# A graph layer with segment maxima: x theta^T of the last 5120 nodes is made in the middle of the kernel and kept in HBM

## The chip, the cores and the metric

One core of one Trainium2 chip runs the whole layer. Its engines are TensorE (PE: matmuls and transposes into PSUM; PEld are its weight loads), VectorE (DVE), ScalarE (ACT), GpSimd (POOL, which also issues the gathers, indirect DMAs), and SyncE (SP, which only issues DMAs here). Each engine works through its own queue in order. The metric is the time of one execution on the device in microseconds (us). A profiled execution gives the trace from which all durations below come.

## The reference

```python
# x (6250, 256), src and dst (100000,), dst ascending; theta_w, phi_w (256, 256)
x_src, x_dst = x[src], x[dst]
e   = relu((x_dst - x_src) @ theta_w.T + theta_b + x_src @ phi_w.T + phi_b)
out = segment_max(e, dst, num_segments=6250)
out = where(isfinite(out), out, 0.0)
x   = layernorm(x + out)           # over the last axis, eps 1e-5
```

All edges of one destination share `x_dst @ theta_w.T` and the biases. With a = x theta^T + both biases (one row per destination) and b = x (phi - theta)^T (one row per source), the result before the layer norm is x + relu(a + max of b over the sources). So no matmul is needed per edge: the work is two products of 6250 x 256 by 256 x 256, and a maximum over 100000 rows of b.

## The kernel before

Nodes are split. Part 1 is the first 1130 nodes (nine tiles of at most 128), part 2 the last 5120 (40 tiles of 128). The edges of part 1 are taken by gathers; those of part 2 partly by matmuls with 0/1 matrices, the rest by gathers again. The stages, with the times they take in the profile:

- **Prep (40 to 148 us).** `x_transposed` (lines 742 to 750) transposes two tiles of x on TensorE and copies them from PSUM with ScalarE into a tile `x_t`; `b_of` (752 to 762) makes b from it, and b goes to HBM (`b_rows`). Meanwhile GpSimd gathers rows of x for the first groups of part 1's edges. `run` (683 to 696) takes running maxima over a group of eight steps on VectorE (line 688) and writes them to HBM (`maxima`, line 696) from SP.
- **Choice (148 to 262 us).** Sources are cut into 17 slots of 383 rows. `choice` (VectorE) picks for each node of part 2 at most one source per slot, `wanted` (1024 to 1031) transposes the picks and writes them to HBM (`chosen_rows`). The loop over `s0`, two slots a turn, also calls `next_group_1(1)`: the gathers of one group of part 1 (`b_rows`, without pauses here, `paced[0] = 0`), one `node_place`, and one fetch part.
- **Fetch parts (85 of them, 165 to 653 us).** `slot_part(s, c)` loads the picks of 1024 nodes (`want`, line 1061), makes 0/1 matrices `hot` from them on ScalarE (lines 1067 and 1068, two instructions a block; from `dve_hots[0] = DVE_HOTS` on, one of three blocks on VectorE, line 1065), and multiplies them with the slot's rows of b on TensorE (line 1075, 24 matmuls of 128 x 512). The results are copied (slot 0, line 1084, ScalarE) or maximised (later slots, line 1086, VectorE) into the accumulator `acc`, 128 x 2 x 5120: column n holds node n's maxima, transposed.
- **List (263 to 646 us).** What the choice left over is gathered from `b_rows`, eight steps a group, a pause (an `iota` of 160 columns, line 488) behind each gather (`paced[0] = 1`); `run` writes its maxima to `maxima_2`. Parts and groups are woven together in a fixed order.
- **End (654 to 744 us).** `rows_of` (1274 to 1319) takes shares of eight tiles, the last two of four: it loads x (`x_f`, ring of `X_RING`), gathers each node's maxima from HBM (line 512), and per piece of two tiles transposes x again (1292), copies it (`x_t`, 1294), makes a with theta and the bias (1299, 1302), for part 2 transposes `acc` back (1309) and takes the maximum with the gathered rows (1310), adds a (1311), and adds relu of it to x with a sum per row (1314). `normalise` (1321 to 1344) is the layer norm: squares on ScalarE (1328), root on both engines (418 to 424), x_f on ScalarE (1338), write of out from SP (1344). A class `Shares` weaves the norm of one share between the pieces of the next. One share of part 1, `LAST`, is done near the end of the fetch already.

Which instruction stands where in an engine's queue is decided by the scheduler of the framework at build time, from the order of the program and the buffers: a tile's ring (`bufs`) sets how many are in flight, and an instruction whose buffer is not free waits at the head of its queue.

Of the kernel before, what the change touches and what calls it, by code (L numbers as in the profile page):

```python
# [40 lines left out]
FP = mybir.dt.float32  # L41
# [6 lines left out]
ALU = mybir.AluOpType  # L48
# [4 lines left out]
P = 128  # L53
BIG2 = 3.0e38
EPS = 1e-5
STEPS = 8
# [17 lines left out]
SLOT_BITS = 9  # L74
P_BITS = 7
EARLY_STEPS = 6
X_RING = 5
STEPS_BITS = 3
OWN_LIST = 288
LIST_CHUNK = 232  # L80
# [2 lines left out]
PAD_WORD = 63 << 14  # L83
CARRY_GROUPS = 5
CARRY_AT = 9
FAR = 1000000.0
GENERAL_STEPS = 17
LOWEST = -1.0e30
# [10 lines left out]
def flat(t, offset, ap):  # L99

    return bass.AP(tensor=t.tensor, offset=t.offset + offset, ap=ap)
# [326 lines left out]
def gnn_kernel(ctx: ExitStack, tc: tile.TileContext, x, src, dst, theta_w, theta_b, phi_w, phi_b, out):  # L428
# [31 lines left out]
    maxima_2 = dram.tile([P * LIST + 1, D], FP, name="maxima_2")  # L460
    src_list = dram.tile([EDGES], I32, name="src_list")
    dst_list = dram.tile([EDGES], I32, name="dst_list")
    list_words = dram.tile([(P + 4) * OWN_LIST], I32, name="list_words")
    chosen_rows = dram.tile([NS, OWN], HF, name="chosen_rows")
    maxima_1t = maxima_1[: P * T1, :].rearrange("(p t) d -> p t d", t=T1)
# [106 lines left out]
    def misc():  # L572
        return ps_misc.tile([P, 2 * D], FP, name="ps")
# [136 lines left out]
    with (  # L710
# [28 lines left out]
                    nc.tensor.transpose(ps[:, 0, k, :], w_in[:, i, c, k * P : (k + 1) * P], ident)  # L739
                nc.vector.tensor_copy(weights[:, :, i, c * P : (c + 1) * P], ps[:, 0])  # L740

        def x_transposed(rows):
            w = rows.shape[1]
            ps = ps_t.tile([P, 2, KC, P], FP, name="ps_xt")
            for h in range(w):
                for k in range(KC):
                    nc.tensor.transpose(ps[:, h, k, :], rows[:, h, k * P : (k + 1) * P], ident)
            x_t = prep.tile([P, 2, KC, P], FP, name="x_t", bufs=3)
            nc.scalar.copy(x_t[:, :w], ps[:, :w])  # L749
            return x_t  # L750

        def b_of(to, rows):

            n = rows.shape[1]
            x_t = x_transposed(rows)
# [14 lines left out]
        for k, share in enumerate(shares(4)):  # L770
            n = share[2]
            x_q = x_in.tile([P, 4, D], FP, name="x_q")
            if share == LAST:
                nc.vector.memset(x_q[:, 0, :], 0.0)
            nc.sync.dma_start(present(x_q, *share), node_rows(x, *share))
            b_sb = b_out.tile([P, 4, D], FP, name="b_sb")
            for i in range(0, n, 2):
                w = min(2, n - i)
                b_of(b_sb[:, i : i + w, :], x_q[:, i : i + w, :])
            nc.scalar.dma_start(node_rows(b_rows, *share), present(b_sb, *share))  # L780
            if k == X_AFTER:
                x_group(of_x[0])
# [32 lines left out]
    place_2 = const.tile([P, TILES], I32, name="place_2")  # L815
    head_i = const.tile([P, 1], I32, name="head_i")
    carry_caps = const.tile([P, 2, P], FP, name="carry_caps")

    def node_place(j):
        cols = columns[:, j // Q1, :]  # L820
# [452 lines left out]
    def rows_of(part, j0, n, ps_tile):  # L1273


        share = part, j0, n
        x_f = x_ring.tile([P, STEPS, D], FP, name="x_f")
        if share == LAST:
            nc.vector.memset(x_f[:, 0, :], 0.0)
        nc.sync.dma_start(present(x_f, *share), node_rows(x, *share))  # L1280
# [2 lines left out]
        for k in range(n):  # L1283
            gather(m[:, k, :], maxima, places[:, j0 + k : j0 + k + 1])
        totals = work.tile([P, STEPS], FP, name="totals", bufs=3)

        def piece(k):
            w = min(2, n - k)
# [12 lines left out]
                    )  # L1301
                nc.tensor.matmul(a[:, i, :], pick, bias_terms, start=False, stop=True)
            some = m[:, k : k + w, :]
            if part == 2:
                ps = ps_tile().rearrange("p (i d) -> p i d", i=2)
                for i in range(w):
                    at = (j0 + k + i) * P
                    for c in range(KC):
                        nc.tensor.transpose(ps[:, i, c * P : (c + 1) * P], acc[:, c, at : at + P], ident)
                nc.vector.tensor_tensor(some, some, ps[:, :w, :], op=ALU.max)  # L1310
            nc.vector.tensor_tensor(some, some, a[:, :w, :], op=ALU.add)
            for i in range(k, k + w):
                y = x_f[:, i, :]
# [2 lines left out]
                )  # L1316
            yield

        return [piece(k) for k in range(0, n, 2)], normalise(part, j0, n, x_f, totals)

    def normalise(part, j0, n, x_f, totals):

# [58 lines left out]
    def fetch_parts(n):  # L1381
        for _ in range(min(n, len(parts))):
            slot_part(*parts.pop(0))

    def next_group_1(n):
        if groups_1:
            i = groups_1.pop(0)
            gathers = gather_group(i, b_rows)
            if i > X_GROUPS:
                run_1(i - 1, gathers)  # L1390
        if todo:
            node_place(todo.pop(0))
        fetch_parts(n)

    fill_table()
    paced[0] = 0
    for s0 in range(0, NS, BATCH_S):
        choice(s0)
        wanted(s0)
        next_group_1(1)  # L1400
    chunk_heads()
    dve_hots[0] = DVE_HOTS
    for i, _ in enumerate(list_pieces()):
# [83 lines left out]
```

## Time and profile before

| what | value |
|---|---|
| time, median of 3 runs (lowest to highest) | 749.13 us (747.54 to 750.01) |
| the profiled execution: time, span | 746.02 us, 744.2 us |
| TensorE busy | 650.4 us, 87% |
| VectorE busy | 641.4 us, 86% |
| GpSimd busy | 604.9 us, 81% |
| ScalarE busy | 492.7 us, 66% |
| moved by DMA | 164.84 MB, mean 221 GB/s |

The span is from the first to the last instruction in the trace; the time around it is 1.8 us. In the rows shown below, a page line by slice has 40 digits, each the busy share of 18.6 us in tenths (PEclk: the granted clock of TensorE in tenths of full speed). A row by window reads: from and to, length, then busy us (and instructions) of PE, PEld, DVE, ACT and POOL, then the granted clock, the busy share of the DMA engines, and GB/s. A row of a group reads: line, engine, operation, output <- input, shape, count | busy us, mean ns of one | idle time in front of them and what ended it. A row in order of time reads: start, duration, engine, line, operation, and in brackets the idle time before it with what ended it ("issue": nothing that the trace shows).

### The profile page before, as it was taken

The page shows a single profiled execution, that of the slowest core. Times are in us where ns is not written, and L with a number is a line of the kernel's source. Part 1 is how long each engine was busy: PE and PEld are TensorE (multiplying, and loading weights), DVE is VectorE, ACT ScalarE, POOL GpSimd, SP SyncE. Part 2 cuts the span into 40 slices and gives each one's busy share as a digit, 9 for nine tenths or more (in the row PEclk, how much of TensorE's full clock was granted, in tenths as well). Part 3 has the DMA queues.
Part 4 walks back from the last instruction along what each step waited for, and adds up shares of the span by engine and source line. Part 5 has one row for each costly group of instructions (what it writes and reads, how often), then busy time and mean ns, then how long its engine had stood idle before and what let it go on. Part 6 is the DMA issues. An engine that isn't in the chain of part 4 may idle for free.

```text
span 744.2 us, 10255 instructions
## 1 busy us (share of the span) xinstructions
PE 650.4 (87%) x3018; PEld 537.3 (72%) x3018; DVE 641.4 (86%) x1197; ACT 492.7 (66%) x700; POOL 604.9 (81%) x843
## 2 busy tenths in 40 slices
PE   1299999939777999999999999999999999589970
PEld 0288888726556788688888888888888888479970
DVE  6699999999997989598889989889799899768871
ACT  0144444459997777688777877877787775037885
POOL 7788987788887778888888888888888888648840
PEclk9599999959999999999999999999999999999995
DMA  6577745584677787968777777768768777625542
GB/s 207 144 244 244 248 159 193 176 286 151 209 239 256 239 254 231 356 211 267 230 235 223 261 243 251 228 223 251 262 205 261 229 222 250 224 101 180 180 173 116
DMA packets 55895, 164.84 MB, mean 221 GB/s; under 512 B 11835, under 2 KB 19796, under 8 KB 48500
## 3 DMA queue, kind: packets, MB, share of 16 engines
q1 hardware_dynamic: 32344, 98.76, 38.1%
q0 software_dynamic: 20944, 57.62, 27.5%
q10 hardware_dynamic: 2540, 7.69, 2.9%
q8 instruction: 27, 0.44, 0.3%
q14 instruction: 40, 0.33, 0.1%
HBM read 101.08 MB, written 63.74 MB: 221 GB/s over the span
## 4 chain that ended last, share of the span: by engine, by line
PE 52%; ACT 11%; DVE 5%; DMA 5%; POOL 3%; issue 2%; DVEq 0%; ACTq 0%; POOLq 0%; SPq 0%
PE ps_f L1075 49%; DMA want<-chosen_rows 4%; POOL g L512 3%; ACT x_f L1338 3%; ACT squares L1328 3%; ACT hot L1067 2%; ACT hot L1068 2%; DVE acc L1086 2%; PE ps_e L1299 1%; ACT acc L1084 1%; DMA g<-b_rows,src 1%; ACT x_t L1294 1%; DVE g L688 1%; DVE x_f L1314 1%; DVE g L1310 0%
## 5 line engine op out<-in xcount | busy, mean ns | idle before, releaser
L1075 PE MATMUL ps_f<-hot,terms 128*128 128x512 f32 x1960 | 458.0, 395 | 29.0 <-ACT hot L1068 15.6
L1075 PEld LDWEIGHTS ps_f<-hot,terms 128*128 128x128 f32 x1960 | 370.2, 190 | 113.1 <-ACT hot L1068 19.8
L512 POOL DMA_INDIRECT g<-b_rows,list_src x232 | 235.4, 1015 | 39.4 <-issue 35.6
L1067 ACT ACTIVATE hot<-want,minus_row 128x1024 fp32r<-128x1024 f16 x169 | 186.2, 1147 | 92.7 <-PE ps_f L1075 80.2
L1086 DVE TENSOR_TENSOR acc<-acc,ps_f 128x1024 f32<-128x1024 f32 x160 | 193.5, 1215 | 31.9 <-PE ps_f L1075 31.0
L688 DVE SCALAR_TENSOR_TENSOR g<-g,caps 128x256 f32<-128x256 f32 x376 | 180.0, 479 | 8.4 <-DMA g<-b_rows,src 5.2
L1068 ACT ACTIVATE hot<-hot 128x1024 fp32r<-128x1024 f32 x169 | 169.1, 1046 | 0.0
L512 POOL DMA_INDIRECT g<-b_rows,src x98 | 128.0, 1306 | 30.5 <-issue 25.3
L488 POOL IOTA pause<- 128x160 f32 x384 | 120.4, 314 | 5.5
L759 PE MATMUL ps_b<-weights,x_t 128*128 128x256 f32 x388 | 90.5, 388 | 1.3 <-ACT x_t L749 0.5
L759 PEld LDWEIGHTS ps_b<-weights,x_t 128*128 128x128 f32 x388 | 72.9, 192 | 14.4 <-ACT x_t L749 5.0
L512 POOL DMA_INDIRECT g<-in_x_dram,src x48 | 60.3, 1256 | 11.3 <-issue 7.1
L512 POOL DMA_INDIRECT g<-maxima,place x49 | 47.6, 972 | 24.6 <-issue 22.5
L1065 DVE TENSOR_SCALAR hot<-want,row_id 128x1024 fp32r<-128x1024 f16 x76 | 59.8, 788 | 6.4 <-DMA want<-chosen_rows 6.3
L1299 PE MATMUL ps_e<-weights,x_t 128*128 128x256 f32 x192 | 48.5, 380 | 0.3 <-ACT x_t L1294 0.2
L1299 PEld LDWEIGHTS ps_e<-weights,x_t 128*128 128x128 f32 x192 | 32.8, 190 | 3.9 <-ACT x_t L1294 0.8
L1294 ACT COPY x_t<-ps_e 128x512 f32<-128x512 f32 x24 | 13.7, 574 | 32.4 <-PE ps_e L1292 32.4
L762 ACT COPY b_sb<-ps_b 128x512 f32<-128x512 f32 (+1 forms) x25 | 14.4, 578 | 29.8 <-PE ps_b L759 28.0
L762 ACT COPY g<-ps_b 128x512 f32<-128x512 f32 x24 | 14.1, 586 | 29.8 <-PE ps_b L759 27.5
L1338 ACT ACTIVATE x_f<-x_f,r 128x256 f32<-128x256 f32 x49 | 25.3, 590 | 10.8 <-DVE r L1335 10.7
L749 ACT COPY x_t<-ps_xt 128x512 f32<-128x512 f32 (+1 forms) x49 | 26.1, 593 | 0.0
L1328 ACT ACTIVATE squares<-x_f,r 128x256 bf16<-128x256 f32 x49 | 24.2, 499 | 1.6 <-DMA g<-b_rows,list_src 1.0
(266 smaller groups left out, 502.2 us busy)
## 6 DMA issues: line engine op xcount, KB each, us to landing
maxima<-g SPq DMA_DIRECT2D x47, 1024.0 KB
want<-chosen_rows SPq DMA_DIRECT2D x85, 256.0 KB
x_q<-in_x_dram SPq DMA_DIRECT2D x12, 512.0 KB
b_rows<-b_sb ACTq DMA_DIRECT2D x12, 512.0 KB
x_f<-in_x_dram SPq DMA_DIRECT2D x5, 1024.0 KB
out_dram<-x_f SPq DMA_DIRECT2D x5, 1024.0 KB
raw<-b_rows SPq DMA_DIRECT2D x16, 256.0 KB
g<-b_rows,list_src POOLq DMA_INDIRECT x232, 4.3
```

The source lines that it names most:

```text
L488: return nc.gpsimd.iota(t, pattern=[[step, t.shape[1]]], base=base, channel_multiplier=per_partition, allow_small_or_imprecise_dtypes=True,)
L512: in_turn(nc.gpsimd.indirect_dma_start(out=out, out_offset=out_offset, in_=in_, in_offset=in_offset))
L688: one = nc.vector.scalar_tensor_tensor(g[:, k, :], last[part], caps[:, t : t + 1], g[:, k, :], op0=ALU.min, op1=ALU.max)
L759: nc.tensor.matmul(ps[:, h, :], x_t[:, h, k, :], weights[:, k, 0, :], start=(k == 0), stop=(k == KC - 1))
L1065: nc.vector.tensor_scalar(hot[:, b, :], want, row_id[:, b : b + 1], None, op0=ALU.is_equal)
L1067: nc.scalar.activation(hot[:, b, :], want, AF.Abs, bias=minus_row[:, b : b + 1], scale=1.0)
L1068: nc.scalar.activation(hot[:, b, :], hot[:, b, :].bitcast(FP), AF.Relu, bias=1.0, scale=-1.0)
L1075: nc.tensor.matmul(ps[:, w : w + 512], terms[:, part, b, h * P : (h + 1) * P], hot[:, b, w : w + 512], start=(i == 0), stop=(i == n - 1),)
L1086: latest_part[0] = nc.vector.tensor_tensor(to, to, ps, op=ALU.max).ins.name
L1299: nc.tensor.matmul(a[:, i, :], x_t[:, 2 * i + c, :], weights[:, c, 1, :], start=(c == 0), stop=False)
L1328: nc.scalar.activation(squares, x_f[:, k, :], AF.Square, bias=mean[:, k : k + 1], scale=1.0, accum_out=var[:, k : k + 1])
L1338: nc.scalar.activation(x_f[:, k, :], x_f[:, k, :], AF.Identity, bias=mean[:, k : k + 1], scale=inv[:, k : k + 1])
```

## The change

The transposed x of part 2's columns is no longer thrown away after b is made. `x_transposed` copies it into the accumulator, whose columns are free until slot 0 writes them. A new function `a_piece` makes a = x theta^T + biases of two tiles from there, copies it with ScalarE to SBUF, and writes it to HBM (`a_rows`) from SP. The loop of the choice calls seven pieces in each of its first turns (7, 7 and 6), behind `wanted` and ahead of `next_group_1`; its first turn makes no fetch part, and one is made behind the loop instead. At the end, `piece_2` takes the place of `piece` for part 2: no transposes of x, no copy, no matmuls with theta; rows of a are loaded from HBM, four tiles at a time into a ring of three, and added from there. To make room the ring of x_f is four, not five. And `paced[0] = 0` takes the pauses away behind the gathers of the end.

```diff
-X_RING = 5
+X_RING = 4
+A_AT_ONCE = 7
+    a_rows = dram.tile([OWN, D], FP, name="a_rows")
...
-        def x_transposed(rows):
+        def x_transposed(rows, tile_at):
...
-            x_t = prep.tile([P, 2, KC, P], FP, name="x_t", bufs=3)
+            if tile_at is None:
+                x_t = prep.tile([P, 2, KC, P], FP, name="x_t", bufs=3)
+            else:
+                x_t = acc[:, :, tile_at * P : (tile_at + w) * P].rearrange("p c (h n) -> p h c n", h=w)
             nc.scalar.copy(x_t[:, :w], ps[:, :w])
...
-                b_of(b_sb[:, i : i + w, :], x_q[:, i : i + w, :])
+                b_of(b_sb[:, i : i + w, :], x_q[:, i : i + w, :], share[1] + i if share[0] == 2 else None)
...
+    def a_piece(j):
+
+        ps = misc().rearrange("p (i d) -> p i d", i=2)
+        for i in range(2):
+            at = (j + i) * P
+            for c in range(KC):
+                nc.tensor.matmul(
+                    ps[:, i, :], acc[:, c, at : at + P], weights[:, c, 1, :], start=(c == 0), stop=False
+                )
+            nc.tensor.matmul(ps[:, i, :], pick, bias_terms, start=False, stop=True)
+        a_sb = work.tile([P, 2, D], FP, name="x_t")
+        nc.scalar.copy(a_sb, ps)
+        nc.sync.dma_start(flat(a_rows, j * D, [[TILES * D, P], [D, 2], [1, D]]), a_sb)
...
-        x_f = x_ring.tile([P, STEPS, D], FP, name="x_f")
+        x_f = x_ring.tile([P, STEPS, D], FP, name="x_f", bufs=X_RING)
...
+        def rows_of_a(k):
+
+            a_f = x_ring.tile([P, STEPS // 2, D], FP, name="a_f")
+            w = min(STEPS // 2, n - k)
+            nc.sync.dma_start(a_f[:, :w, :], flat(a_rows, (j0 + k) * D, [[TILES * D, P], [D, w], [1, D]]))
+            return a_f
+
+        a_tiles = [rows_of_a(k) for k in range(0, n, STEPS // 2)] if part == 2 else []
+
+        def piece_2(k):
+            w = min(2, n - k)
+            yield
+            some = m[:, k : k + w, :]
+            ps = ps_tile().rearrange("p (i d) -> p i d", i=2)
+            for i in range(w):
+                at = (j0 + k + i) * P
+                for c in range(KC):
+                    nc.tensor.transpose(ps[:, i, c * P : (c + 1) * P], acc[:, c, at : at + P], ident)
+            nc.vector.tensor_tensor(some, some, ps[:, :w, :], op=ALU.max)
+            q, at = divmod(k, STEPS // 2)
+            nc.vector.tensor_tensor(some, some, a_tiles[q][:, at : at + w, :], op=ALU.add)
+            for i in range(k, k + w):
+                y = x_f[:, i, :]
+                nc.vector.scalar_tensor_tensor(
+                    y, m[:, i, :], 0.0, y, op0=ALU.max, op1=ALU.add, accum_out=totals[:, i : i + 1]
+                )
+            yield
...
-            if part == 2:
...
-        return [piece(k) for k in range(0, n, 2)], normalise(part, j0, n, x_f, totals)
+        return [(piece if part == 1 else piece_2)(k) for k in range(0, n, 2)], normalise(part, j0, n, x_f, totals)
...
     fill_table()
+    a_pieces = list(range(0, TILES, 2))
     paced[0] = 0
     for s0 in range(0, NS, BATCH_S):
         choice(s0)
         wanted(s0)
-        next_group_1(1)
+        for _ in range(min(A_AT_ONCE, len(a_pieces))):
+            a_piece(a_pieces.pop(0))
+        next_group_1(1 if s0 else 0)
+    fetch_parts(1)
     chunk_heads()
...
-    x_ring = body.enter_context(tc.tile_pool(name="x_ring", bufs=X_RING, side="right"))
+    x_ring = body.enter_context(tc.tile_pool(name="x_ring", bufs=3, side="right"))
...
     last_shares += [(2, j, STEPS // 2) for j in (TILES - STEPS, TILES - STEPS // 2)]
+    paced[0] = 0
     at_end = Shares(lambda: ps_end.tile([P, 2 * D], FP, name="ps_e"))
```

More of the change, by code (lines that the diff above doesn't have):

```diff
@@ L747, in x_transposed, with b_of @@
                     nc.tensor.transpose(ps[:, h, k, :], rows[:, h, k * P : (k + 1) * P], ident)
-            x_t = prep.tile([P, 2, KC, P], FP, name="x_t", bufs=3)
+            if tile_at is None:
+                x_t = prep.tile([P, 2, KC, P], FP, name="x_t", bufs=3)
+            else:
+                x_t = acc[:, :, tile_at * P : (tile_at + w) * P].rearrange("p c (h n) -> p h c n", h=w)
             nc.scalar.copy(x_t[:, :w], ps[:, :w])
             return x_t
-        def b_of(to, rows):
+        def b_of(to, rows, tile_at=None):
             n = rows.shape[1]
-            x_t = x_transposed(rows)
+            x_t = x_transposed(rows, tile_at)
             ps = ps_b.tile([P, 2, D], FP, name="ps_b")
@@ L1303, in piece @@
             some = m[:, k : k + w, :]
-            if part == 2:
[L1305 to L1310, printed above, removed]
             nc.vector.tensor_tensor(some, some, a[:, :w, :], op=ALU.add)
```

## The prediction

> **What bounds the kernel now.** I read the page's busy shares by slice first, then a table by window, then the groups and the order of time of the last 80 us, then the choice stage on ScalarE, SyncE and GpSimd.
>
> ```profile
> PE   1299999939777999999999999999999999589970
> ACT  0144444459997777688777877877787775037885
> PEclk9599999959999999999999999999999999999995
> ```
>
> TensorE is full nearly everywhere, with two holes: 148 to 262 us (the choice stage) and 620 to 655 us (the end of the fetch). ScalarE fills the first hole. The busy time of each engine by window:
>
> ```profile
> 147.60:262.00 114.40, 84.77 (x334) 63.98 (x334) 107.56 (x211) 94.52 (x142) 94.51 (x74) 0.90 0.73 234
> 300.00:320.00 20.00, 18.43 (x80) 14.30 (x79) 11.66 (x16) 14.23 (x16) 17.82 (x27) 1.00 0.92 332
> 320.00:620.00 300.00, 300.00 (x1325) 248.39 (x1325) 267.37 (x388) 233.73 (x233) 266.00 (x398) 1.00 0.75 239
> 620.00:655.00 35.00, 25.19 (x109) 19.72 (x108) 30.63 (x52) 7.16 (x10) 22.84 (x36) 0.95 0.59 200
> ```
>
> Between 320 and 620 us TensorE has no idle time at all: whatever it loses before, it cannot win back there. In the hole before it is idle for 114.4 - 84.8 = 29.6 us, and it waits 1.6 us at 300 to 320.
>
> Groups of instructions from 665 us on, and the order of time on GpSimd (choice stage, then end) and ScalarE (last rows):
>
> ```profile
> L1299 PE MATMUL ps_e<-weights,x_t 128*128 128x256 f32 x161 | 40.7, 380 | 0.1
> L512 POOL DMA_INDIRECT g<-maxima,place x37 | 35.4, 958 | 7.7 <-issue 5.8 <-DVE r L424 1.9
> L1314 DVE SCALAR_TENSOR_TENSOR x_f<-g,x_f 128x256 f32<-128x256 f32 x42 | 16.2, 422 | 0.5
> L1310 DVE TENSOR_TENSOR g<-g,ps_e 128x512 f32<-128x512 f32 x20 | 13.7, 687 | 6.1 <-PE ps_e L1309 6.0
> L1294 ACT COPY x_t<-ps_e 128x512 f32<-128x512 f32 x19 | 10.8, 571 | 4.8 <-PE ps_e L1292 4.8
> ```
>
> ```profile
> 224.89 0.96 POOL L512 DMA_INDIRECT g<-b_rows,src  x1 [0.30 <-issue]
> ...
> 660.81 0.95 POOL L512 DMA_INDIRECT g<-maxima,place  x1 [15.07 <-issue]
> 661.77 0.28 POOL L488 IOTA pause<- 128x160 f32 x1
> 662.21 0.95 POOL L512 DMA_INDIRECT g<-maxima,place  x1 [0.16 <-issue]
> ...
> 717.77 0.95 POOL L512 DMA_INDIRECT g<-maxima,place  x1 [0.16 <-issue]
> ```
>
> ```profile
> 726.49 6.00 ACT L1338 ACTIVATE x_f<-x_f,r 128x256 f32<-128x256 f32 x12 [0.52 <-DVE r L1335]
> ...
> 736.39 2.07 ACT L1338 ACTIVATE x_f<-x_f,r 128x256 f32<-128x256 f32 x4 [1.23 <-DVE r L1335]
> ```
>
> From 654 to 722 us TensorE is full again: a piece of two tiles costs 2.84 us (four transposes of x 0.44, eight L1299 and two L1302 matmul records 1.96, four transposes of acc 0.44). But the gathers need 1.41 us each (0.95, pause, issue) and run to 718.7; VectorE adds its last rows at 724.6, and ScalarE has 14 us of squares and x_f behind it, to 738.5. So TensorE is the first of three nearly equal limits there.
>
> **End of the kernel, part by part.** Gone from each of 20 pieces: 2.40 us of TensorE (48.0 in all), and the x_t copy, 0.47 us on ScalarE when chained (9.4). What is late next:
> - GpSimd. Without a pause a gather takes 0.96 + 0.30 = 1.25 us (row 224.89), so 40 take 50 instead of 56.4 us. They start when the last maxima are in HBM, 660.8, which the change leaves alone; the last one starts at 660.8 + 39 x 1.25 = 709.6 and, at 3.0 us to landing, is there at 712.6.
> - VectorE. A piece is max 0.72, add 0.72, two sums 0.71: 2.2 us (674.0 to 676.2 in its order of time); mean and root add some 1.9 us a share of eight tiles. That is 10.7 us a share against TensorE's 11.4. Five shares from 666 us end near 720, not 724.6: a gain of only 4 us.
> - ScalarE. Eight squares at 0.49 and eight x_f at 0.50 are 8 us a share, but they follow the share's sums and VectorE's chain of root steps (2.0 us), and both queues are in order. In the emitted order of the changed kernel the sums of the last four tiles stand behind the root of the third share from the end, and ScalarE's squares of the next share wait for x_f of the one before. I walked both queues with these durations. The third-last share's squares end at 716.7; then root 2.2, x_f 4.0, five squares 2.5, root 2.3, x_f 4.0, root and two squares of the last shares 1.5, x_f 2.0, two squares 1.0, root 2.2, x_f 2.0: 740.4. The same walk on the kernel before gives 741.2 where the trace has 738.5. With that bias the end of the kernel gains about nothing: I take +1 us, with -3 (the whole bias off) and +5 (gathers at 1.41 after all) as ends.
> - Added: ten loads of rows of a (512 KB) on SP. One waits for the buffer's last reader and stands in front of the writes of out and the loads of x_f. With one x_f buffer fewer, the last x_f waits for the write of share B, whose x_f is done at 713.8: it lands by 719 to 722, 0 to 3 us late, inside the 5 above.
>
> **The choice stage, part by part.** Each of the 20 a_pieces costs TensorE 1.96 us: 39.2 us. Idle there are 29.6, so TensorE comes out of the stage at least 9.6 us later even if packed without a gap. With the 1.6 us of 300 to 320 that is +8.0, the low end.
>
> The queues say that it will not be packed. ScalarE is busy 18.6 to 20 of each 20 us from 160 to 220, and gets 20 copies of 0.47 to 0.57 us, 7 of them ahead of the first hot. In SP's order five writes of a_rows now stand in front of the first want, issued at 155.46 before. The fourth needs the buffer of the second, which is issued behind the maxima of 155.02, and itself goes behind the maxima of 161.67: want at 162.8, 7.3 us later. Then 13 more copies (6.5), three node_place moved behind (3.3), and near 197 us one more buffer wait of 4 us (a_rows issued behind maxima at 196.4, landing some 4 later, between the 3.1 and 6.5 that the chain shows for a want of the same 256 KB). So ScalarE has its 54th hot near 254, not 232, and TensorE its 216th fetch matmul near 254.5, not 240.5: +14. After that TensorE's waits of 1.2, 0.6 and 1.6 us are covered: +10.5. Nine parts are still made before dve_hots rises, so the part moved behind the loop costs nothing. I take +9.5 between +8 and +10.5. In 620 to 655 TensorE is idle for 9.8 us; most moves along (VectorE's in-order maxima, the want behind LAST's write of out), but up to 4 us may be absorbed. At the other end a_rows' 5.2 MB can cost 5 us more in gathers. Ends: +4 and +16.
>
> The Trainium skill (TensorE: Matmul & The Clock Gate, Part 1) says an array idle for some 3.4 us falls to half clock. The granted clock of 0.80 and 0.78 in 140 to 180 agrees. By it the a_pieces would keep TensorE warm: an estimate of up to 2 us less, were those matmuls not waiting for ScalarE. The Trainium skill (DMA: Bandwidth & Descriptors, Anatomy of one DMA) prices a transfer at 2.0 us plus bytes over 436 GB/s, most of it the receipt of the write, longest in HBM. For 256 KB its estimate is 2.6 us instead of my 4, which takes about 1 us off; no run here shows such a write.
>
> **Elsewhere.** 20 of the x_t copies in the prep stage go into acc in four pieces of 128: 0.59 us as now, while ScalarE is half idle there (TensorE 19.9 of 20 us), so 0 up to a doubled price. SP's 30 more issues at 0.32 us lie between waits.
>
> **Sum.** 9.5 + 1 = +10.5 us. The profiled execution took 746.0 (span 744.2, 1.8 around it), so 756.5; the median of the runs lies 3.1 higher, so 759.6.
>
> **Rivals.** (1) *Faster: ScalarE's relief shortens the tail.* If ScalarE is never behind VectorE, its 9.4 us come off the tail behind a VectorE that ends 4 us earlier: -13, with +9 ahead: 745. For it: 14 us of ScalarE behind the last sum. Against: ScalarE is idle 4.8 us for x_t alone, and the order binds the two queues. It decides if the third-last share's x_f are done before the last sums. (2) *The moved work is hidden*: the choice stage absorbs all but what 620 to 655 takes back: 749 to 751. Against: 39.2 is more than 29.6. (3) *Gathers without pauses crawl.* In 140 to 262 us unpaused gathers took 1.33 us on average plus 0.30, some 3.75, with DMA 0.73 busy; the end now adds 5.2 MB of a to its traffic. At 1.63 the last gather starts at 724.4 and the end goes +12: 771. Against: 1.25 flat from 222 to 234 at a share of 0.8.
>
> **How the numbers follow.** Forecast 0.55 (alone 753 to 766), rival 1 0.20, rival 2 0.10, rival 3 0.15. The range 745 to 772 leaves half of rival 1 and a third of rival 3 out. Within 0.3% (2.2 us; about what a measurement of this kernel can tell from no change) lies rival 2. Faster 0.20, same 0.10, slower 0.70.
>
> **What would show it.** Right: first hot near 169, TensorE solid from about 262, first ps_e near 664, gathers 1.25 us apart, VectorE's last sum some 57 us behind the first ps_e, ScalarE the last engine. Wrong: ps_e before 658 (the stage packs better than its idle time), or ScalarE's end under 80 us behind the first ps_e (the walk of the tail fails), or gathers over 1.4 us.

## The result and the profile after

The changed kernel takes 787.75 us (median of 4 runs, 786.0 to 793.0), the kernel before 749.0 (747.5 to 750.0): 1.053 times as long, 95% interval 1.0485 to 1.0576. Beside a later experiment it took 784.6 against 750.9: 1.045, 1.040 to 1.050. A ratio compares only runs within 1.5% of the fastest of the same kernel. The forecast was 759.6 with a range of 745 to 772: slower was right, the size was not.

The page of the changed kernel, three rows of its 40 slices (19.6 us each):

```profile
PE   1399999969974799999999999999999999683200
ACT  0144444338784896687787787777877777024486
PEclk9999999989996899999999999999999999995555
```

The ninth to eleventh slices, 157 to 216 us, are fuller than before, but a new hole stands in the twelfth to fourteenth, 216 to 275 us, and at the end TensorE has little to do.

The table by window of the changed kernel, with the columns busy time of TensorE, of its weight loads, of VectorE, ScalarE and GpSimd, then granted clock, DMA share and GB/s. The first row is cut as in the prediction, the others at 140, 220, 340 and 600 us and at the first ps_e, where the end stage begins:

```profile
147.60:262.00 114.40, 87.24 (x377) 70.08 (x375) 84.84 (x157) 71.12 (x122) 95.47 (x68) 0.90 0.76 254
140.00:220.00 80.00, 70.85 (x331) 59.12 (x330) 74.31 (x138) 48.11 (x87) 69.60 (x40) 0.96 0.76 260
220.00:340.00 120.00, 97.70 (x412) 77.16 (x411) 79.42 (x175) 89.00 (x110) 80.38 (x99) 0.93 0.69 226
340.00:600.00 260.00, 260.00 (x1149) 215.26 (x1148) 226.56 (x323) 203.59 (x204) 230.76 (x343) 1.00 0.73 233
600.00:690.04 90.04, 81.33 (x352) 65.99 (x350) 81.48 (x129) 51.05 (x55) 62.51 (x91) 0.98 0.68 220
690.04:784.60 94.56, 26.45 (x136) 20.68 (x136) 54.75 (x207) 51.53 (x155) 39.35 (x40) 0.59 0.56 197
```

and the kernel before, cut the same way:

```profile
140.00:220.00 80.00, 56.51 (x224) 42.32 (x223) 78.75 (x150) 64.69 (x109) 67.77 (x46) 0.87 0.68 218
220.00:340.00 120.00, 112.00 (x484) 89.81 (x483) 100.75 (x202) 90.92 (x98) 99.42 (x126) 0.99 0.79 256
600.00:654.38 54.38, 44.57 (x191) 35.67 (x190) 48.59 (x79) 23.32 (x27) 40.66 (x62) 0.97 0.65 216
654.38:744.20 89.82, 67.16 (x416) 61.44 (x416) 58.93 (x207) 61.65 (x175) 49.90 (x80) 0.90 0.46 155
```

Three things are to be read here. The first ps_e came at 654.38 and comes at 690.04: 35.7 us of the 40.4 us between the two spans are lost by the end of the fetch, and the end itself grew from 89.8 to 94.6. From 340 to 600 us TensorE has no idle time in either kernel. And its idle time from 140 to 340 is the same: 23.5 + 8.0 = 31.5 us before, 9.15 + 22.3 = 31.45 us after. The pieces filled 14.3 us of the first hole, and 14.3 us opened behind it. So the pieces' TensorE time came on top: its busy time up to the first ps_e rose by 36.7 us, from 583.2 to 619.9.

The new hole in SyncE's order of time (start, duration, and what it issues):

```profile
203.35 1.16 SPq L1080 DMA_DIRECT2D want<-chosen_rows  x1
...
217.26 9.72 SPq L698 DMA_DIRECT2D maxima<-g  x2
227.08 0.38 SPq L1050 DMA_DIRECT2D chosen_rows<-rows  x1
227.55 1.06 SPq L1080 DMA_DIRECT2D want<-chosen_rows  x1
237.78 0.32 SPq L698 DMA_DIRECT2D maxima<-g  x1
...
247.15 0.32 SPq L698 DMA_DIRECT2D maxima<-g  x1
247.56 0.38 SPq L1080 DMA_DIRECT2D want<-chosen_rows  x1
257.56 0.32 SPq L698 DMA_DIRECT2D maxima<-g  x1
...
258.59 1.14 SPq L1080 DMA_DIRECT2D want<-chosen_rows  x1
```

and the same stretch in the kernel before:

```profile
221.30 0.32 SPq L696 DMA_DIRECT2D maxima<-g  x1
224.32 0.32 SPq L1061 DMA_DIRECT2D want<-chosen_rows  x1
...
230.72 0.32 SPq L696 DMA_DIRECT2D maxima<-g  x1
231.21 0.32 SPq L1061 DMA_DIRECT2D want<-chosen_rows  x1
```

From 217 on a write of maxima goes every 10 us, because its run waits for eight gathers that GpSimd issues 1.25 us apart, and each of these wants stands right behind such a write. The kernel before has the same pattern there, but by 220 us it had issued eight wants, the changed kernel five. VectorE's waits, 140 to 340 us, the changed kernel and then the kernel before (us in total, times, longest):

```profile
DVE g L690 <- DMA g<-b_rows,src: 25.4, 21, 4.8
```

```profile
DVE g L688 <- DMA g<-b_rows,src: 5.2, 5, 2.4
```

VectorE's queue has the same fault. Counted in its emitted order (its order of time gives the same), 96 run steps (`g L688`, one running maximum each) stood before the first sum of the fetch into acc in the kernel before; in the changed kernel 127 do (`g L690`). That sum ran at 215.2 us before and runs at 257.4 now. From 220 to 260 us GpSimd issues gathers without a break, while VectorE is busy 18.0 us of 40 and TensorE 22.1 (the changed kernel, then the kernel before):

```profile
220.00:260.00 40.00, 22.10 (x81) 16.43 (x80) 17.96 (x38) 25.77 (x41) 30.43 (x32) 0.79 0.69 221
220.00:260.00 40.00, 33.57 (x140) 25.99 (x139) 34.23 (x79) 30.56 (x37) 31.00 (x32) 0.96 0.77 240
```

Behind that, GpSimd waits 19.9 us for VectorE's run_start, which the list needs and for which it did not wait before; the list's first gather goes at 304.2 us, 277.2 before.

The end of the changed kernel. First its gathers on GpSimd, then VectorE's waits from the first ps_e on, then the longest pieces of its chain there, then ScalarE's last row:

```profile
696.44 0.94 POOL L514 DMA_INDIRECT g<-maxima,place  x1 [24.72 <-DMA maxima<-g]
697.69 0.95 POOL L514 DMA_INDIRECT g<-maxima,place  x1 [0.30 <-issue]
...
746.73 0.95 POOL L514 DMA_INDIRECT g<-maxima,place  x1 [0.30 <-issue]
```

```profile
DVE g L1324 <- DMA g<-maxima,place: 12.2, 8, 2.4
DVE r L1373 <- ACT squares L1368: 8.0, 4, 3.1
DVE x_f L1329 <- DMA x_f<-in_x_dram: 2.6, 1, 2.6
```

```profile
713.35 3.30 DMA g<-maxima,place
721.42 3.48 DMA g<-maxima,place
739.20 6.72 DMA g<-maxima,place
750.27 3.93 ACT x_f L1378 x8
```

```profile
777.68 2.07 ACT L1378 ACTIVATE x_f<-x_f,r 128x256 f32<-128x256 f32 x4 [1.24 <-DVE r L1375]
```

The gathers do come 1.25 us apart (the last starts 50.3 us behind the first, 39 gaps of 1.29 on average), but they land a median of 3.9 us after issue instead of 3.0, VectorE now waits for that, as it did not in the kernel before, and once it waits for the last share's x_f.

### The profile page after: what moved, and what is told of

Same layout as the page of the kernel before. It is cut to its first block, busy times and chain, and to the rows that moved or that the text cites. A ratio compares the mean times of both kernels' runs of the same rounds, so it can differ in the third digit from the quotient of the medians.

```text
span 784.6 us, 10102 instructions
## 1 busy us (share of the span) xinstructions
PE 646.4 (82%) x2938; PEld 531.3 (68%) x2938; DVE 639.9 (82%) x1197; ACT 493.7 (63%) x700; POOL 600.3 (77%) x795
## 4 chain that ended last, share of the span: by engine, by line
PE 44%; POOL 10%; DMA 10%; DVE 8%; ACT 5%; issue 5%; SPq 0%; DVEq 0%; POOLq 0%; ACTq 0%
PE ps_f L1094 43%; POOL g L514 9%; DMA want<-chosen_rows 4%; DMA g<-b_rows,src 3%; DVE acc L1105 2%; ACT x_f L1378 2%; DMA g<-maxima,place 2%; DVE g L690 2%; ACT squares L1368 1%; DMA a_rows<-x_t 1%; ACT hot L1086 1%; DVE hot L1084 1%; ACT hot L1087 0%; DMA maxima<-g 0%; POOL dst_w L514 0%
## 5 line engine op out<-in xcount | busy, mean ns | idle before, releaser
L1094 PE MATMUL ps_f<-hot,terms 128*128 128x512 f32 x1960 | 455.3, 393 | 14.4 <-ACT hot L1087 7.2
L1105 DVE TENSOR_TENSOR acc<-acc,ps_f 128x1024 f32<-128x1024 f32 x160 | 193.6, 1215 | 36.4 <-PE ps_f L1094 35.7
L690 DVE SCALAR_TENSOR_TENSOR g<-g,caps 128x256 f32<-128x256 f32 x376 | 180.5, 480 | 28.8 <-DMA g<-b_rows,src 25.4
L514 POOL DMA_INDIRECT g<-b_rows,src x98 | 135.3, 1381 | 29.9 <-issue 25.2
L490 POOL IOTA pause<- 128x160 f32 x336 | 105.2, 313 | 5.2
L764 PE MATMUL ps_b<-weights,x_t 128*128 128x256 f32 x228 | 53.0, 386 | 0.6
L830 PE MATMUL ps<-weights,acc 128*128 128x256 f32 x160 | 43.2, 401 | 8.1 <-ACT x_t L835 7.1
L764 PEld LDWEIGHTS ps_b<-weights,x_t 128*128 128x128 f32 x228 | 42.7, 192 | 8.3 <-ACT x_t L754 2.7
L830 PEld LDWEIGHTS ps<-weights,acc 128*128 128x128 f32 x160 | 28.9, 200 | 13.5 <-ACT x_t L835 8.6
L764 PE MATMUL ps_b<-weights,acc 128*128 128x256 f32 x160 | 36.8, 383 | 0.2
L1323 PE MATMUL ps_e<-ident,acc 128*128 128x128 f32 x80 | 16.5, 362 | 22.6 <-DVE g L1324 22.6
L764 PEld LDWEIGHTS ps_b<-weights,acc 128*128 128x128 f32 x160 | 29.7, 190 | 5.1 <-ACT acc L754 1.3
L767 ACT COPY b_sb<-ps_b 128x512 f32<-128x512 f32 (+1 forms) x25 | 14.5, 578 | 29.4 <-PE ps_b L764 29.4
```

The costliest lines, as they stand in the source:

```text
L490: return nc.gpsimd.iota(t, pattern=[[step, t.shape[1]]], base=base, channel_multiplier=per_partition, allow_small_or_imprecise_dtypes=True,)
L514: in_turn(nc.gpsimd.indirect_dma_start(out=out, out_offset=out_offset, in_=in_, in_offset=in_offset))
L690: one = nc.vector.scalar_tensor_tensor(g[:, k, :], last[part], caps[:, t : t + 1], g[:, k, :], op0=ALU.min, op1=ALU.max)
L764: nc.tensor.matmul(ps[:, h, :], x_t[:, h, k, :], weights[:, k, 0, :], start=(k == 0), stop=(k == KC - 1))
L830: nc.tensor.matmul(ps[:, i, :], acc[:, c, at : at + P], weights[:, c, 1, :], start=(c == 0), stop=False)
L1094: nc.tensor.matmul(ps[:, w : w + 512], terms[:, part, b, h * P : (h + 1) * P], hot[:, b, w : w + 512], start=(i == 0), stop=(i == n - 1),)
```

## Experiments

Two theories at first. *Queue*: wants of the fetch stand on SyncE behind the writes of a_rows and maxima. *TensorE*: 39 us of matmuls stand in front of the fetch. Later two forms of an answer: *runs in front* (parts of the fetch wait in several in-order queues behind runs that the gathers pace) and *one for one* (TensorE's time comes on top whatever the order).

### One part of the change at a time

The pieces alone, with the old end (a_rows is written and never read):

```diff
-X_RING = 4
+X_RING = 5
-a_tiles = [rows_of_a(k) for k in range(0, n, STEPS // 2)] if part == 2 else []
+a_tiles = []
-return [(piece if part == 1 else piece_2)(k) for k in range(0, n, 2)], normalise(part, j0, n, x_f, totals)
+return [piece(k) for k in range(0, n, 2)], normalise(part, j0, n, x_f, totals)
-paced[0] = 0
 at_end = Shares(lambda: ps_end.tile([P, 2 * D], FP, name="ps_e"))
```

(The edit is shown in part: piece also has its transposes of acc and their maximum back, and the pool has its old size, as in the kernel before.)

> Leaves out the change of the end: x theta^T of the slots' columns is made and written as in the changed kernel, but the end transposes x, multiplies it by theta and paces its gathers as before; a_rows is never read. After's fetch ended 35.6 us later than before's and its end stage took 4.8 us longer. If the choice stage carries the loss as the two traces say: 780 to 786 us, the first ps_e near 690 us. If the end is to blame for more than it seems (its rows and gathers collide with something): under 775.

783.0 us against 752.4: 1.040 (1.031 to 1.050); first ps_e at 695.3. The end alone:

```diff
-for _ in range(min(A_AT_ONCE, len(a_pieces))): a_piece(a_pieces.pop(0))
-next_group_1(1 if s0 else 0)
+next_group_1(1)
-nc.sync.dma_start(a_f[:, :w, :], flat(a_rows, ...))
+nc.sync.dma_start(a_f[:, :w, :], node_rows(x, 2, j0 + k, w))
```

(x_transposed also puts its copy into a tile of its own again.)

> The change of the end alone: no pieces are made beside the choice, and the end adds rows of x where the changed kernel adds rows of a_rows (same bytes, same layout; x theta^T is left out of the sum for the slots' columns). If the end costs what the traces say: the fetch ends near 654 us and the whole takes 751 to 757. By the prediction's term of +1: 750. If unpaced gathers hold the maxima back: above 760.

757.5 us against 752.4: 1.008 (1.004 to 1.012). First ps_e at 657.8, end stage 94.6 us as in the changed kernel. The two ratios add up to 1.049, inside the 1.045 to 1.053 of the whole change. With intervals of some 1% on the first, an interaction of a few us between the parts could not be seen.

The end's pauses by themselves, in the kernel before:

```diff
+paced[0] = 0
 at_end = Shares(lambda: ps_end.tile([P, 2 * D], FP, name="ps_e"))
```

> The kernel before with its last 48 gathers unpaced and nothing else: 47 pauses of 0.16 us go, the gathers come 1.25 us apart instead of 1.41. If VectorE's sums follow the gathers: 744 to 748. If the gathers' landings slow down as the queue fills, 749 to 757 as in the run with the end alone (757.5 beside a before of 752.4).

753.8 us against 752.3: 0.9995 (0.996 to 1.003); its end stage took 89.4 us. Gathers without pauses are worth nothing there, and alone they are not what made the end longer: they land after a median of 2.8 us, while those of the end alone land after 3.9. What is left for the 4.7 us are the rows read back and the smaller ring of x_f. The ring was tried alone:

```diff
-X_RING = 5
+X_RING = 4
```

> The kernel before with 4 buffers for x_f instead of 5, and nothing else. In the changed kernel's end the last share's x_f lands 2.6 us after VectorE wants it, behind the second share's write, and the end stage is 4.8 us longer. If the ring causes that: the end stage grows from 89.8 to 92 or more and the whole by 2 to 5 us. If not: no change, within 3 us.

824.3 us against 818.8 on a chip where every kernel took longer (below): 1.012 (1.004 to 1.021). But its end stage was 116.8 us there, against 118.9 for a kernel with five buffers (`f8`, below) on the same chip. So its excess lies elsewhere than in the end, and this run does not settle the ring.

### The pieces, taken apart

Copies and writes without the matmuls, and matmuls and copies without the writes:

```diff
-nc.tensor.matmul(ps[:, i, :], acc[:, c, at : at + P], weights[:, c, 1, :], start=(c == 0), stop=False)
-nc.tensor.matmul(ps[:, i, :], pick, bias_terms, start=False, stop=True)
-nc.scalar.copy(a_sb, ps)
+nc.scalar.copy(a_sb, weights[:, :, 1, :])
```

> The changed kernel without the 200 matmuls of the pieces: ScalarE copies weights in their place, a_rows is written and read as in the changed kernel (x theta^T is left out). Theory 'queue' (wants of the fetch stand on SyncE's queue behind a_rows and maxima writes): most of the loss stays, 770 to 785. Theory 'TensorE' (42 us of matmuls stand in front of the fetch): the loss of the choice stage falls to what the moved first part costs, 750 to 760.

777.3 us against 752.4: 1.035 (1.027 to 1.042). This was the surprise. Without any of TensorE's 39 us most of the loss stayed, as 'queue' said.

```diff
-nc.sync.dma_start(flat(a_rows, j * D, ...), a_sb)
```

(Here and in the next one the end reads rows of x in the place of a's.)

> The changed kernel with the matmuls and ScalarE's copies but without the 20 writes of a_rows; the end reads rows of x instead (the x theta^T sum is left out). Theory 'queue' or 'traffic' (5.2 MB of writes and 20 places on SyncE's queue): 752 to 765. Theory 'TensorE': 780 to 788, the fetch ends near 690 as after.

782.6 us: 1.040 (1.033 to 1.048). Without any write most of the loss stayed too, as 'TensorE' said. The last one has neither copies nor writes:

```diff
-a_sb = work.tile([P, 2, D], FP, name="x_t")
-nc.scalar.copy(a_sb, ps)
-nc.sync.dma_start(flat(a_rows, j * D, ...), a_sb)
```

> The 200 matmuls of the pieces alone: no copies to SBUF, no writes (x theta^T is left out of the result), the end adds rows of x. Theory 'one for one': 39 us of TensorE with the holes as they are, the first ps_e at 685 or later, 776 to 788. Theory 'ScalarE' (copies that wait for landings hold the hots back): 757 to 768, since TensorE's pieces then fill holes as was forecast.

778.2 and 787.3 us, 1.043 (1.034 to 1.052) of a before of 749.9; two more runs took 792.3 and 792.5. The matmuls are enough alone. What writes and ScalarE's copies add on top of them is within the intervals, 1.043 beside 1.045 and 1.053 with everything.

How can the matmuls and everything but the matmuls each cost most of it? Both put the fetch late by 220 us (94 of its matmuls begun in the run with the matmuls alone, 109 in the run without them, 164 in the kernel before), and behind that a similar thing happens. ScalarE's longest waits of the run without matmuls, 140 to 340 us:

```profile
ACT hot L1078 <- DMA want<-chosen_rows: 23.9, 5, 14.8
ACT junk L839 <- PE ps L836: 8.7, 5, 5.2
```

The 14.8 us are one want that went at 250.65, behind maxima writes of 239.07 and 249.80. In that run too, 124 run steps stand before VectorE's first sum, and 127 in the run with the matmuls alone.

### The moved part, the bursts

```diff
-next_group_1(1 if s0 else 0)
-fetch_parts(1)
+next_group_1(1)
```

> The changed kernel with one part undone: every turn of the choice has its part of the fetch, the first turn too, and none is made up behind the loop. Theory 'moved part' (the part that waits until the loop is over sets the wants back): 760 to 772. Theories 'wants behind maxima' and 'pieces in front': the fetch still ends near 690, 780 to 790.

786.5 us against 752.3: 1.043 (1.034 to 1.051); the moved part is not the main cause. Moved alone in the kernel before:

```diff
-next_group_1(1)
+next_group_1(1 if s0 else 0)
 ...
+fetch_parts(1)
 chunk_heads()
```

> The kernel before with the moved part alone: the first turn of the choice has no part of the fetch, one is made behind the loop; no pieces, the old end. Theory 'moved part': 760 or more. Otherwise within 6 us of before, 746 to 755.

758.1 us: 1.008 (1.003 to 1.013). Some 6 us, between the two expectations. Whether it adds to the pieces these intervals cannot tell.

```diff
-A_AT_ONCE = 7
+A_AT_ONCE = 4
-next_group_1(1 if s0 else 0)
-fetch_parts(1)
+next_group_1(1)
```

> The changed kernel with 4 pieces in a turn instead of 7 (five turns instead of three), and a part of the fetch in every turn. In the changed kernel the rows of chosen nodes of turns 2, 3 and 4 leave at 171.9, 194.7 and 212.5 us, before at 156.5, 159.0 and 185.7: the 7 pieces of a turn stand between two of them on TensorE and ScalarE. Theory 'rows behind pieces': smaller bursts let the rows out sooner, TensorE's idle time of 140 to 340 us falls from 31.5 to some 20, 770 to 778. Theory 'one for one' (the holes are waits that matmuls in front only move, so the 39 us of TensorE come on top): idle time near 30, 781 to 790.

788.2 us against 749.9: 1.052 (1.047 to 1.058). The rows came out sooner as expected (162.9, 182.4, 198.2 us instead of 171.9, 194.7, 212.5), and it helped nothing: idle time 6.3 us at 140 to 220, but 24.3 at 220 to 340. TensorE's largest wait there:

```profile
PE ps_f L1094 <- DVE acc L1105: 16.7, 1, 16.7
```

It waits for a sum that VectorE has behind its runs. 'Rows behind pieces' falls.

### Off SyncE's queue

```diff
-nc.sync.dma_start(want, ...)
+nc.scalar.dma_start(want, ...)
```

> The changed kernel with the wants of the fetch issued by ScalarE's queue instead of SyncE's, so that none stands behind a write of maxima or of a_rows. Theory 'wants behind maxima': the hole of TensorE at 220 to 280 us (21 us) closes by half or more, 757 to 772. Theory 'pieces in front' (the order on TensorE and ScalarE): 780 to 792. Slower than 792 if the issues cost ScalarE more than they give.

796.8 us against 752.3: 1.061 (1.055 to 1.068), no faster than the changed kernel. With the rows of chosen nodes moved as well, in the changed kernel and in the kernel before:

```diff
-nc.sync.dma_start(flat(chosen_rows, s0 * OWN, ...), rows[:n])
+nc.scalar.dma_start(flat(chosen_rows, s0 * OWN, ...), rows[:n])
-nc.sync.dma_start(want, ...)
+nc.scalar.dma_start(want, ...)
```

> The changed kernel with both the rows of chosen nodes and the wants issued by ScalarE's queue; SyncE's keeps a_rows and maxima. In the run with the wants alone on ScalarE's queue the rows still stood behind maxima writes (rows 0.4 us behind a write at 222.0, 253.5). Theory 'behind maxima': with both away the hole at 220 to 280 us closes by half or more, the first ps_e comes before 680, 768 to 778. Theories 'rows behind pieces' and 'one for one': no better than the changed kernel, 783 to 797.

> The kernel before with the rows of chosen nodes and the wants on ScalarE's queue. If writes of maxima in front of wants make TensorE's 31.5 us of idle time at 140 to 340: 735 to 747. If the fetch is held by VectorE's and GpSimd's order: 750 to 760.

798.4 us (1.064, 1.059 to 1.068) and 765.4 us (1.019, 1.013 to 1.025) against 749.9, the second slower than either expectation. SyncE's queue is not the cause by itself. TensorE's two longest waits at 140 to 340 us in the first of them:

```profile
PE ps L878 <- DVE capped L879: 14.7, 1, 14.7
PE ps L844 <- DVE hot L842: 8.6, 2, 6.6
```

Both wait for VectorE, whose order still has 127 run steps in front. The edit also puts the issues in ScalarE's order, so it does not price SyncE's queue cleanly.

### The order of VectorE

The next edit leaves all work in place and adds one rule of order: a run of the first maxima stands behind the newest part of the fetch.

```diff
-if part == 2 and latest_part[0] is not None:
+if latest_part[0] is not None:
     behind_in_order(one, latest_part[0], "VectorE's order")
```

> The changed kernel with one more rule of order: the steps of a run of the first maxima (VectorE) stand behind the newest part of the fetch, as those of the list's runs do already, so that their writes stand behind more of the wants on SyncE's queue too. In the changed kernel some 35 run steps, which wait for GpSimd's gathers 1.25 us apart, stand on VectorE in front of the first sum of the fetch, and TensorE idles 17.9 us of 220 to 260. Theory 'runs in front' (parts of the fetch wait in three queues behind runs that GpSimd's gathers pace): TensorE's idle time of 140 to 340 us falls from 31.5 to under 20, the first ps_e comes at 678 or before, 765 to 776. Theory 'one for one' (TensorE's 39 us come on top whatever the order): 781 to 790.

> The kernel before with that same rule of order. Theory 'runs in front': part of its own 31.5 us of idle time at 140 to 340 us goes, 735 to 746. If before's order has no run that holds a part for long: 747 to 753. Slower if the runs themselves come late and hold gathers and the list back.

> The kernel before with that rule and with the turn's part of the fetch emitted ahead of its run instead of behind it. Theory 'runs in front': 732 to 745, no worse than the rule alone. If the order is not the cause: 747 to 755.

(`f8` also emits fetch_parts(n) ahead of run_1 in next_group_1.) These three and the ring of four ran on a chip where the kernel before took 808.9 to 841.2 us. The first took 839.5 (1.029, 1.022 to 1.036), the second 837.1 (1.024, 1.017 to 1.030), the third 818.0 (1.001, 0.996 to 1.006). So in the kernel before the rule left fewer run steps in front of the first sum, 87 and with both edits 79 for 96, and neither version was faster. The trace of the first cannot be used for the question: in its order of time on VectorE stands

```profile
265.83 0.29 DVE L841 TENSOR_SCALAR hot<-columns,low 128x128 f32<-128x128 f32 x1 [41.27 <-remote]
```

a wait of 41.3 us with no releaser on this core. All four traces made on that chip have such waits, no other trace has one, so they do not decide for or against the order. The first was run again on another chip, beside the changed kernel itself:

> The changed kernel with the runs of the first maxima behind the newest part of the fetch, once more, beside the changed kernel itself on the same chip, because the run before was full of stalls (one of 41 us on VectorE) whose cause the profile does not show. Theory 'runs in front': at least 8 us faster than the changed kernel beside it; on a chip where before takes 750, 765 to 778, TensorE's idle time of 140 to 340 us under 22. Theory 'one for one': within 5 us of the changed kernel. Third way: slower than the changed kernel, because the runs come late and hold GpSimd's gathers and the list back; the first gather of the list then starts after 304.

> The changed kernel itself, as the measure for the run beside it: 1.05 times before, 784 to 793 on a chip where before takes 750.

777.9 us (773.6 to 780.0) against 784.6 (782.3 to 786.6) and a before of 750.9: ratios 1.033 (1.027 to 1.038) and 1.045 (1.040 to 1.050), which do not overlap. The windows of the run with the rule, then of the changed kernel beside it:

```profile
140.00:220.00 80.00, 71.23 (x335) 59.86 (x334) 72.55 (x134) 48.77 (x88) 70.82 (x36) 0.96 0.72 246
220.00:340.00 120.00, 109.93 (x471) 88.08 (x470) 88.93 (x189) 99.68 (x122) 82.46 (x98) 0.97 0.73 243
600.00:683.71 83.71, 70.28 (x291) 56.10 (x289) 69.03 (x110) 40.89 (x44) 65.20 (x96) 0.92 0.63 213
```

```profile
140.00:220.00 80.00, 70.63 (x329) 58.65 (x328) 74.78 (x139) 47.97 (x87) 69.14 (x42) 0.96 0.76 266
220.00:340.00 120.00, 100.31 (x429) 79.49 (x428) 81.13 (x177) 92.48 (x115) 82.44 (x101) 0.94 0.69 226
600.00:685.59 85.59, 77.42 (x335) 62.76 (x334) 77.78 (x122) 48.51 (x52) 59.06 (x86) 0.98 0.64 219
```

The rule halves the hole at 220 to 340 us, 19.7 to 10.1 us; the idle time of both windows, 18.8 us, is under the 22 that 'runs in front' asked for. In its emitted order 95 run steps stand before the first sum, and that sum runs at 242.2 instead of 255.1. So the order is a cause of the hole. Which queue carries it is not separated: the rule moves SyncE's order too, where 12 writes of maxima now stand in front of the seventh, eighth and ninth want instead of 15, 16 and 16 (10, 11 and 12 in the kernel before). And the profiled first ps_e comes only 1.9 us sooner: idle time behind 600 us grows from 8.2 to 13.4, where the last of the list's gathers now goes at 663.5 instead of 656.2, although the first goes sooner, at 296.4 instead of 301.7. (The profiled execution took 780.0 us with the rule, above that median of 777.9, and 782.3 without it, below that of 784.6.) The 6.8 us between the medians is under the 8 us that 'runs in front' asked for and over the 5 us of 'one for one'.

### All together

Idle time of TensorE in two windows, run steps of the first maxima in front of VectorE's first sum (counted in the emitted order), when that sum ran, and the first ps_e (us):

| kernel | idle 140-220 | idle 220-340 | run steps | first sum | first ps_e | ratio |
|---|---|---|---|---|---|---|
| before | 23.5 | 8.0 | 96 | 215.2 | 654.4 | 1 |
| end alone | 23.4 | 9.4 | 96 | 215.3 | 657.8 | 1.008 |
| unpaced end | 26.6 | 10.5 | 96 | 218.8 | 665.4 | 1.000 |
| moved part alone | 26.1 | 14.5 | 98 | 222.4 | 669.4 | 1.008 |
| rows, wants on ScalarE, in the kernel before | 29.7 | 19.5 | 107 | 231.6 | 676.2 | 1.019 |
| no matmuls | 32.7 | 16.3 | 124 | 246.1 | 678.1 | 1.035 |
| changed | 9.2 | 22.3 | 127 | 257.4 | 690.0 | 1.053 |
| changed, second trace | 9.4 | 19.7 | 127 | 255.1 | 685.6 | 1.045 |
| matmuls alone (trace of a 792.5 us run) | 8.2 | 26.8 | 127 | 262.7 | 696.0 | 1.043 |
| pieces alone | 8.5 | 22.3 | 127 | 259.9 | 695.3 | 1.040 |
| no writes | 7.1 | 22.4 | 127 | 252.6 | 686.6 | 1.040 |
| first part kept | 6.5 | 21.5 | 127 | 254.8 | 688.0 | 1.043 |
| 4 at once | 6.3 | 24.3 | 127 | 257.3 | 686.7 | 1.052 |
| wants on ScalarE | 8.7 | 29.5 | 127 | 253.0 | 700.2 | 1.061 |
| rows, wants on ScalarE | 8.6 | 37.2 | 127 | 263.1 | 703.9 | 1.064 |
| runs behind parts | 8.8 | 10.1 | 95 | 242.2 | 683.7 | 1.033 |

Every version with the pieces, whole or in part, and without the rule of order lets 124 or 127 run steps pass VectorE before the fetch's first sum, matmuls or not. With the work and without that order (runs behind parts) the loss is 1.033; with that order and without the matmuls it is 1.035; with both 1.045 to 1.053; the end's 0.8% is in each. The two overlap, since each sets the same fetch late. So the rule, which puts the order right, takes back 6.8 us of 33.7; the larger share stays with the work itself. What stays open: how much the order costs with nothing else changed (without the matmuls the copies and writes were still there), and why, with the runs behind the parts, the list's gathers start 5 us sooner and end 7 us later. No kernel tried is faster than the kernel before.

## Why the prediction was wrong

**The sum's first term, +9.5 for the choice stage, measured +35.7.** The step that failed is the walk of the queues that sized this term: "TensorE its 216th fetch matmul near 254.5, not 240.5: +14". That matmul came at about 279, 39 us later. The bound ahead of it, at least 9.6 us "even if packed without a gap", held, but the term was then set next to the bound, as if nearly all idle time of the stage were room. The cost of a piece was right, 1.96 us where pieces ran one behind another. The holes, however, are waits. By 220 us the pieces had filled 14.3 of 23.5 idle us. What stood behind them then ran into a supply set by the gathers, and the same 14.3 us came back at 220 to 340.

**Where the walk of the queues broke.** I walked SyncE and ScalarE in the new order and kept the times of the maxima writes and VectorE's order as they were. The first steps came out near: first want at 165.5 for 162.8, first hot at 173.0 for 169. From there on the walk was blind to the 31 more run steps in front of VectorE's first sum. By 220 us five wants had been issued, eight before, and the list's first gather went 27 us later. TensorE was solid from 272, not 262, but for 1.2 us. That the place of the runs causes half of the idle time at 220 to 340 is shown by the run with the rule; whether it accounts for more of the loss is open.

**The low end, +4, and the 4 us absorbed at 620 to 655**: neither happened. Idle time from 600 us to the first ps_e was 9.8 us before and 8.7 us after.

**Nine parts are still made, so the moved part costs nothing**: in the changed kernel right, within what can be measured; alone in the kernel before it costs some 6 us.

**a_rows' traffic, up to 5 us in gathers; a buffer wait of 4 us.** Landings of 5.5 and 4.4 us stand in the chain of waits:

```profile
164.02 5.52 DMA a_rows<-x_t
170.25 4.35 DMA a_rows<-x_t
...
247.56 6.23 DMA want<-chosen_rows
253.81 2.19 ACT hot L1086 x2
```

ScalarE waited for such landings 19.0 us in all at 140 to 220, not 4; yet without the writes 1.040 was left of 1.045 to 1.053, so the traffic as such is not most of the loss. The Trainium skill (DMA: Bandwidth & Descriptors, Anatomy of one DMA) gives its price for DMAs that GpSimd issues, and a_rows goes through SyncE's queue. The estimate of 2.6 us by it was too low for the 5.52 and 4.35 us of these writes; the measurement decides.

**The clock.** The pieces did keep TensorE warm: its granted clock at 140 to 220 rose from 0.87 to 0.96. By the Trainium skill (TensorE: Matmul & The Clock Gate, Part 1) a busy array gets its full clock, and the trace agrees. What it gained is small, since the hole behind, at 220 to 260, ran at 0.79 instead of 0.96: the fetch's 1960 matmuls kept TensorE busy 455.3 us instead of 458.0.

**The end, +1 with -3 and +5 as ends, measured +4.7.** Gathers 1.25 apart: right. The term that was mis-sized is their landing, taken as 3.0 us: the median is 3.9, and it took 6.72 us for the gather of 739.20, at a DMA share of 0.83 in 720 to 740, where rows of a and x are loaded and a write of out runs beside it. The squares of the third-last share end at 757.5, 5 us behind the walk's 716.7 moved by 35.7. The x_f of the last share was 2.6 us late, inside the 0 to 3 forecast. VectorE's last sum came 73.2 us behind the first ps_e (70.3 before). The 57 us named in the forecast was a slip: its own sum, 720 + 9.5 against 664, gives 65.5, and that was missed as well, because the gain of 4 us on VectorE did not come. The end alone, which reads rows of x in their place, has the same 12.2 us of waits and the same median of 3.9, and the unpaced end, which reads none, has no such wait. So the new end brings the late landings and the missing pauses alone do not; that it is the rows read back and not the smaller ring is an argument from the DMA share.

**The rivals.** ScalarE's relief (1) did not shorten the tail: ScalarE waited 12.3, 11.2 and 9.7 us for VectorE's root and mean there. The work was not hidden (2), and the gathers did not crawl (3): they took 1.29 us each on average. None of the three was the case that came, a second hole behind the first. It should have been a rival, with the 31 more steps that the emitted order shows as its evidence.

## What to carry to other kernels

An engine's idle time inside a stage is room only if the stage's supply does not depend on what is put there: ask of each hole what it waits for, and whether that wait comes later when the hole is filled. Where a scheduler writes the queues, compare its order before and after on every engine, the ones the change does not touch first, and count what now stands in front of the critical kind of instruction. Then put a rule of order on it and measure: where two causes are each enough, removing one at a time makes neither look like a cause.

## What the runs showed that was not expected

- The pieces' matmuls alone (1.043), and their copies and writes without the matmuls (1.035), were each enough for most of the loss, beside 1.045 to 1.053 with everything.
- Executions with the same instructions up to the end (before, end alone, unpaced end) reached the first ps_e at 654.4, 657.8 and 665.4 us. By 220 us GpSimd had issued 60, 58 and 52 of the 98 gathers from b_rows for part 1; in the last of them three gathers took over 5 us each (longest 9.8), in the first none (longest 3.8). An effect of under some 11 us on the first ps_e is not to be read from one trace.
- One chip took 819 us for the kernel that others ran in 750. In the traces made there VectorE waited 54 to 79 us in all, and ScalarE 36 to 83, for releases that no record on the core explains; in the traces made elsewhere there are none. What holds them is open.
- Moving the issue of 85 wants and nine writes of rows from SyncE's queue to ScalarE's made both kernels slower, by 1 to 2%, though ScalarE is busy only 63% of the changed kernel's span.
